# A neighbour-quantile graph kernel: other instructions for the degree classes, another direction of the stepped access in the long lists' keys, and two list steps on ScalarE instead of VectorE

## The chip, the cores and the metric

The kernel runs on one core of a Trainium2 chip. The metric is the device time of one execution in microseconds (us); lower is better. The engines are called as in the profile: PE is TensorE (PEld its weight loads), DVE is VectorE, ACT is ScalarE, POOL is GpSimd, SP is SyncE.

## What is computed

There are 16 graphs of 1024 nodes with 64 channels, a weighted adjacency of 1024 x 1024 for each, and two layers. The first adds a degree-normalised product of the adjacency with the normalised features. The second drops some neighbours, takes weighted quantiles over those that stay, for every node and channel, and puts the result through a two-layer MLP:

```python
h = jnp.maximum(_layernorm(x, axis=-1), 0.0)
x = x + _L0_gnn_ref(h, adj)            # (adj / clip(rowsum, 1)) @ h
h = jnp.maximum(_layernorm(x, axis=-1), 0.0)
x = x + _L1_gnn_ref(h, adj, nodemask, W1, b1, W2, b2)

# inside _L1_gnn_ref
nb = (adj_ > 0) & (~eye)[None]
m = nb.sum(-1)
rank = jnp.cumsum(nb, axis=-1) - 1
skip = jnp.where(m > T_THRESH, (m + K_DIL - 1) // K_DIL, 1)
removed = nb & do_dil[..., None] & ((rank + 1) % skip[..., None] == 0)
rem = removed | jnp.swapaxes(removed, 1, 2)
adj_d = jnp.where(rem, 0.0, adj_)
agg = _weighted_nanquantile_agg(x, adj_d > 0)    # quantiles 0.25, 0.5, 0.75 with weights 0.25, 0.5, 0.25
out = x + agg
h = jax.nn.relu(jnp.einsum('bnc,ch->bnh', out, W1) + b1)
y = (jnp.einsum('bnh,ho->bno', h, W2) + b2) * mask
```

The adjacency is sparse: most nodes have fewer than 16 neighbours, a few have up to some 90.

## The kernel before

**List path.** Sorting 1024 values for every node and channel would be wasteful, so the kernel makes a list of neighbours for every node, gathers their feature rows, and sorts the gathered values with a network of pairwise minima and maxima on DVE. A second path for dense graphs (`dense_path`) stands behind a condition and isn't taken with these inputs.

**First stage, a batch (graph) at a time.** The adjacency rows come in by DMA (`at`). ACT takes their sign with a row sum (`sg`, `total`). DVE multiplies the sign with a descending key and takes the eight largest keys in each of four segments (`rec`, 32 entries of a row, a 0 where there is none). PE transposes the rows and multiplies them with the features, ACT and DVE normalise. Then `endings` sorts the nodes of the batch by the length of their lists. Each node gets a class `d` from 0 to 22: below 16 it is the number of entries found; above, one more for each limit in `STEPS` that `total` passes; a full segment of eight makes it at least 16. The class is compared with a table of all classes (`cls`) to a one-hot `hot` of 23 x 8 entries, and PE products and a scan on DVE turn `hot` into places. POOL then scatters the rows of the nodes to these places in DRAM (`srt`) by indirect DMA.

**Second stage, a group at a time.** `GROUPS` makes four groups of four batches. `group(g)` reads the sorted records, drops the neighbours that the rule removes, and opens a `Job` for each class of lists: 15, 10 and 8 entries (one tile of 128 nodes each), 7 (two tiles), 6 (one tile), and 5 to 1 entries (four to six tiles). A job gathers one neighbour of 128 nodes with each indirect DMA on POOL (`places<-tab,idx`; for the last group `places<-tab,last_idx`). `sort` then finds the dropped places by comparison (`rem`, `gone`, `ok`), adds 1e30 times `gone` to their values in one DVE instruction so that they sort to the end, and runs the passes of the network. ACT takes the absolute value and the rectifier of the weights (`wu`, in `steps`). `weigh` multiplies the sorted values, which stand in one of two buffers (`places` is copy 0, `other` is copy 1), with the weights on DVE, one instruction for each run of places. For a short list the products go into `prod`. PE sums them by products with an identity (`pt`), then come the MLP on PE and ACT, one addition a tile on DVE (`y`), and a scatter to the output on POOL. The last group's tiles have names with `last_`; its jobs start once all batches are through.

**Long lists.** Eight rows of each batch have lists of up to 88, 28, 21 and 18 entries (`LONG`). `long_lists` makes, for each of the four, a row of keys in 16 bits (`lkey`): 1024 descending keys (`rev`) where the adjacency is positive, else 0. The instruction reads in the order of the columns and writes into eight segments, so that consecutive elements lie 128 elements, 256 bytes, apart. Searches in the segments (`lfound`, `lkeys`) give the indices for the gathers (`lplaces<-whole,lidx`). The first of the four (tag `l0`) is sorted in blocks by code of its own (`parts`, `merge`).

**Order of work.** It is written out at build time by a planner. Every piece of work is a Python generator (a stream) that yields the engine that it wants next, and when its inputs are ready. `Plan.run` always takes the stream that can start first by its own clocks and ranks; `Plan.note` moves the clocks by a cost for each instruction. A DVE instruction costs 0.07 us + 1.04 ns an element in it, an ACT instruction 0.06 us + 0.86 ns an element + 0.11 us for each bias or scale that is a pointer. The planner knows nothing of steps in memory. `SLACK` (2 us), `LOOSE` (7) and `LATE` (14) are distances that it leaves between a result and its reader. On the chip each engine runs its instructions in the written order[...].

In the trace nearly all instructions carry line 240, the planner's recording helper, so they are told apart by tile names.

Of the kernel before, what the change touches and what calls it, by code (L numbers as in the profile page):

```python
# [26 lines left out]

GROUPS = (4, 4, 4, 4)
NSEG = 4
STEPS = (16, 19, 22, 29, 39, 59, 79)  # L30
CLS = 15 + len(STEPS) + 1

# [353 lines left out]
def list_path(ctx, tc, x, adj, nodemask, w1, b1, w2, b2, out, go):  # L386
# [51 lines left out]
    nc.vector.memset(zero_f, 0.0)  # L438
    place1 = consts.tile([P, P], F32, name="place1")
    nc.vector.tensor_scalar(place1, col[:, :P], 1.0, None, op0=OP.add)  # L440
    cls_i = grp.tile([P, N], I32, name="gat_rows", bufs=1)[:, :CLS * NT]
    cls_i = cls_i.rearrange("p (c t) -> p c t", t=NT)
    nc.gpsimd.iota(cls_i, pattern=[[-1, CLS], [0, NT]], base=CLS - 1, channel_multiplier=0)
    cls = consts.tile([P, CLS, NT], F32, name="cls")
    nc.vector.tensor_copy(cls, cls_i)
    row_i = consts.tile([P, NT], I32, name="row_i")
    nc.gpsimd.iota(row_i, pattern=[[P, NT]], base=0, channel_multiplier=1)
    row_f = consts.tile([P, NT], F32, name="row_f")
# [323 lines left out]
    def endings(pool, now):  # L772

        first = lambda rank: rank - 3000
        for b, st in enumerate(batch):
            now[0] = b
            g = max(g for g in range(NG) if FIRST[g] <= b)
            size = GROUPS[g]
            yield "ACT", lambda: known(st, "rec", "row") if st["listed"] == NT else INF
            rec, total, row = st["rec"], st["total"], st["row"]  # L780

            for t in range(NT):
                nc.scalar.activation(
                    row[:, t, R0:R0 + 8 * NSEG], rec[:, t, :], AF.Relu, bias=before[:, t:t + 1]
                )


            yield "DVE", always
            found = new(pool, [P, NT, 8 * NSEG], BF, "found", 1)
            nc.vector.tensor_scalar(found, rec, 0.0, None, op0=OP.is_gt)  # L790
            d = new(tiny, [P, NT], F32, "d", 2)
            nc.vector.tensor_reduce(d, found, AX.X, OP.add)
            full = new(tiny, [P, NT], F32, "full", 2)
            nc.vector.tensor_reduce(
                full, found.rearrange("p t (s e) -> p t s e", e=8)[:, :, :, 7], AX.X, OP.max
            )
            nc.vector.scalar_tensor_tensor(d, full, float(STEPS[0]), d, op0=OP.mult, op1=OP.max)
            nc.vector.tensor_scalar(d, d, float(STEPS[0]), None, op0=OP.min)
            for s in STEPS[1:]:
                nc.vector.scalar_tensor_tensor(d, total, float(s), d, op0=OP.is_gt, op1=OP.add)  # L800
            free(rec)
            free(total)
            hot = new(tiny, [P, CLS, NT], BF, "hot", 2)
            nc.vector.tensor_tensor(
                hot, cls, d.unsqueeze(1).to_broadcast([P, CLS, NT]), OP.is_equal
            )
            yield "PE", lambda: max(at(hot), room("ps_small", 3))
            pc = new(ps_s, [P, HALF], F32, "ps_small", 3, users=1)
            K = CLS * NT
# [12 lines left out]
            pos = new(tiny, [P, NT], F32, "pos", 2)  # L822
            nc.vector.tensor_reduce(pos, base.rearrange("p (c t) -> p t c", t=NT), AX.X, OP.add)
            low = new(tiny, [P, NT], I32, "low", 2)
            nc.vector.tensor_copy(low, pos)
            nc.vector.tensor_scalar(low, low, LSUB - 1, None, op0=OP.bitwise_and)
            if size == 2:
                aside = new(tiny, [P, 2, NT], F32, "aside", 2)
                for e, by in enumerate((-32.0, 64.0)):
                    nc.vector.tensor_scalar(  # L830
                        aside[:, e, :], pos, 64.0 / (e + 1), by, op0=OP.is_lt, op1=OP.mult
                    )
                for e in range(2):
# [12 lines left out]
            progress["batches"] = b + 1  # L846
# [23 lines left out]
    class Job:  # L870
# [185 lines left out]
        def steps(self):  # L1056
            nc.scalar.activation(self.u, self.u, AF.Abs)
            nc.scalar.activation(self.u, self.u, AF.Relu, bias=wt0, scale=-QUANTILES[0][1])

        def merge(self):  # L1060
            self.counts(self.ok)
            yield "ACT", lambda: at(self.u) + SLACK
            self.steps()
            yield "DVE", always, self.later
            yield from self.passes(len(self.ops) - 1, self.landed)
            yield from self.weigh()

        def sort(self):
# [14 lines left out]
            self.ops, self.count, self.copies = network(n, T * C, one=T == 1)  # L1083
            self.counts(ok)

            vals = A[:, 1:, :, :].rearrange("p k t w -> p (k t) w")[:, :, :C]
            nc.vector.scalar_tensor_tensor(
                vals,
                gone.rearrange("p k t -> p (k t)").unsqueeze(2).to_broadcast(
                    [P, (n - 1) * T, C]  # L1090
                ),
                HUGE, vals, op0=OP.mult, op1=OP.add,
            )
            free(gone)
            yield "ACT", lambda: at(self.u) + SLACK
            self.steps()
            yield "DVE", lambda: max(
                room("prod", 2) if short else 0.0,
                room(name + "other", 1),
            ), self.later  # L1100
            if short:
# [8 lines left out]
        def weigh(self):  # L1110
# [12 lines left out]
            if short:  # L1123
                prod = new(pool, [P, T, total, C], F32, "prod", 2, users=1)
                if count + 1 < total:
                    nc.vector.memset(prod[:, :, count + 1:, :], 0.0)

            for copy in (1, 0):
                mine = [k for k in range(count) if copies[k] == copy]
                for run in runs_of(mine):  # L1130
                    first, step, number = run[:3]
                    sl = slice(first, first + step * (number - 1) + 1, step)
                    src = places(copy, run)
                    nc.vector.tensor_tensor(
                        prod[:, :, sl, :].rearrange("p t k c -> p k t c") if short else src, src,
                        w[:, sl, :].unsqueeze(3).to_broadcast([P, number, T, C]), OP.mult,
                    )
            if short:
                free(A)
                free(Bt)  # L1140
                yield "ACT", lambda: at(S)
                nc.scalar.copy(prod[:, :, count, :], S[:, :, :C])
                free(S)

                terms = [
                    [prod[:, t, k:min(k + 2, total), :].rearrange("p k c -> p (k c)")
                     for k in (0, *range(4, total, 2), 2)]
                    for t in range(T)
                ]
                plan.add(self.layers(terms, [prod]), self.urgent)  # L1150
            else:
                terms = [[places(copies[k], (k, 1, 1, 1, 1))[:, 0, 0, :] for k in range(count)]
                         + [S[:, 0, :C]]]
                plan.add(self.layers(terms, [A, Bt]), -1000)
# [278 lines left out]
    def long_lists(pool):  # L1433

        yield "DVE", always
        rev = new(pool, [P, N], HF, "rev", 1)
        nc.vector.tensor_scalar(rev, col_f, -1.0, float(N), op0=OP.mult, op1=OP.add)
        yield "SP", always
        place = new(pool, [P, 1], I32, "lplace", 1)
        nc.vector.tensor_scalar(place, part, 7, None, op0=OP.bitwise_and)  # L1440
# [17 lines left out]
        for l in LORDER:  # L1458
# [17 lines left out]
            key = new(pool, [P, N], HF, "lkey", 1)  # L1476
            segs = key.rearrange("p (s q) -> p s q", s=LSEG)
            nc.vector.scalar_tensor_tensor(
                segs.rearrange("p s q -> p q s"), full.rearrange("p (q s) -> p q s", s=LSEG), 0.0,
                rev.rearrange("p (q s) -> p q s", s=LSEG), op0=OP.is_gt, op1=OP.mult,  # L1480
            )

            found = new(pool, [P, LSEG, max(LCAPS)], HF, "lfound", 1)
# [395 lines left out]
```

## Time and profile before

| what | value |
|---|---|
| median of 3 runs | 1413.34 us (1410.7 to 1415.0) |
| profiled execution | 1414.18 us, span 1412.4 us |
| DVE busy | 1228.7 us (87%), 4150 instructions |
| POOL busy | 963.8 us (68%), 1115 instructions |
| PE busy | 738.8 us (52%) |
| ACT busy | 557.6 us (39%), 1603 instructions |
| chain that ended last | DVE 46%, POOL 18%, issue 10%, PE 10%, DMA 9%, ACT 6% |

The first stage runs to about 860 us, with the groups' work mixed in from 195 us on; the rest is the remaining groups and the long lists. In the rows of the profile, `out<-in` names the tiles, `xN` is the number of instructions, then come the busy time in us, the mean in ns of one, and the idle time of the engine just before them with what ended it. "issue" is time in which an engine waited for nothing that the profile shows.

### The profile page before, as it was taken

To read this page: it belongs to the slowest core of one execution; us is meant where nothing else is said; L and a number is where in the kernel's file an instruction comes from. 1 tells how busy PE (TensorE), PEld (TensorE's weight loads), DVE (VectorE), ACT (ScalarE), POOL (GpSimd) and SP (SyncE) were. 2 spreads that over 40 slices of the span, in tenths; PEclk is the share of its full clock that TensorE was granted. 3 is DMA by queue.
4 is the path that set the end of the run, shared out by engine and by line. 5 is a ranking of instruction groups with operands and counts; after the bars stand their busy time and mean duration, and the time that the engine had idled before them with its cause. 6 is when DMAs were issued, how large, how long until landed. Compare 5 with 4: busy or idle time off the path is not lost.

```text
span 1412.4 us, 14420 instructions
## 1 busy us (share of the span) xinstructions
PE 738.8 (52%) x3203; PEld 458.2 (32%) x3203; DVE 1228.7 (87%) x4150; ACT 557.6 (39%) x1603; POOL 963.8 (68%) x1115
## 2 busy tenths in 40 slices
PE   4878726376677657839856652002002232337685
PEld 2434413243443335425442331001001121226455
DVE  6999898999888898998999668886998899998985
ACT  6889763765554356865653520000000110001010
POOL 0042347777775787776778877775877777787764
PEclk9999868687787868968966865555555555557566
DMA  5464582443444245545541324211111111111110
GB/s 174 156 195 163 182 228 76 133 154 90 124 107 136 69 119 170 150 142 148 158 125 46 85 46 84 73 44 46 32 25 24 25 34 26 25 28 40 25 25 16
DMA packets 133834, 132.31 MB, mean 94 GB/s; under 512 B 99444, under 2 KB 102132, under 8 KB 133620
## 3 DMA queue, kind: packets, MB, share of 16 engines
q1 hardware_dynamic: 102220, 91.13, 21.8%
q0 software_dynamic: 31520, 40.19, 11.7%
q8 instruction: 27, 0.44, 0.1%
q14 instruction: 67, 0.55, 0.1%
HBM read 111.76 MB, written 23.61 MB: 96 GB/s over the span
## 4 chain that ended last, share of the span: by engine, by line
DVE 46%; POOL 18%; issue 10%; PE 10%; DMA 9%; ACT 6%; SPq 0%; DVEq 0%; POOLq 0%; ACTq 0%
POOL places L240 14%; DVE places L240 8%; DVE rec L240 6%; DVE other L240 5%; PE ps_small L240 5%; PE pt L240 5%; DVE lplaces L240 4%; DVE sg L240 2%; DMA at<-in_adj_dram 2%; DMA places<-tab,idx 2%; DVE l0other L240 2%; ACT sg L240 2%; POOL srt L240 2%; DVE prod L240 2%; DVE lkey L240 1%
## 5 line engine op out<-in xcount | busy, mean ns | idle before, releaser
L240 POOL DMA_INDIRECT places<-tab,idx x372 | 375.8, 1010 | 121.2 <-issue 104.2
L240 PE MATMUL pt<-ident,prod 128*128 128x128 f32 (+1 forms) x736 | 152.2, 367 | 385.8 <-DVE prod L240 330.9
L240 PE MATMUL ps_small<-att,h 128*65 128x512 f32 x512 | 261.7, 662 | 77.3 <-ACT h L240 55.9
L240 PEld LDWEIGHTS pt<-ident,prod 128*128 128x128 f32 (+1 forms) x736 | 126.0, 252 | 418.0 <-DVE prod L240 248.6
L240 POOL DMA_INDIRECT srt<-row,to x128 | 131.6, 1028 | 140.0 <-ACT row L240 118.9
L240 PE MATMUL pt<-ident,at 128*128 128x128 f32 x1024 | 164.0, 304 | 72.0 <-ACT att L240 52.7
L240 DVE MAX8 rec<-sg 128x8 f16<-128x256 f16 x512 | 180.2, 414 | 4.4
L240 ACT ACTIVATE sg<-at 128x1024 f16<-128x1024 f32 x128 | 134.8, 1054 | 102.0 <-DMA at<-in_adj_dram 65.6
L240 POOL DMA_INDIRECT lplaces<-whole,lidx x125 | 146.8, 1174 | 38.1 <-issue 36.9
L240 ACT COPY ot<-pt 128x128 f32<-128x128 f32 (+3 forms) x56 | 22.4, 400 | 377.4 <-PE pt L240 377.2
L240 PEld LDWEIGHTS pt<-ident,at 128*128 128x128 f32 x1024 | 125.7, 155 | 113.9 <-ACT att L240 77.6
L240 POOL DMA_INDIRECT places<-tab,last_idx x124 | 135.0, 1089 | 37.8 <-issue 35.0
L240 ACT COPY att<-pt 128x512 f32<-128x512 f32 x256 | 140.7, 584 | 26.8 <-PE pt L240 25.3
L240 PEld LDWEIGHTS ps_small<-att,h 128*65 128x65 f32 x512 | 76.1, 155 | 220.9 <-issue 125.0
L240 POOL DMA_INDIRECT out_dram<-y,nodes_i x93 | 95.7, 1029 | 20.6 <-issue 12.7
L240 DVE TENSOR_TENSOR sg<-sg,keyed 128x1024 f16<-128x1024 f16 x128 | 87.4, 682 | 15.6 <-ACT sg L240 15.6
L240 ACT ACTIVATE wu<-wu 128x39 f32<-128x39 f32 (+9 forms) x40 | 9.4, 235 | 152.0 <-DVE wu L240 152.0
L240 PE MATMUL ps_small<-ot,w_sb 128*128 128x128 f32 (+3 forms) x112 | 52.0, 554 | 30.8 <-DVE base L240 11.9
L240 DVE TENSOR_TENSOR places<-places,other 128x128 f32<-128x128 f32 (+6 forms) x160 | 56.4, 355 | 3.4
L240 PE MATMUL ps_small<-w_sb,hid 128*128 128x64 f32 x256 | 50.1, 332 | 1.9 <-ACT hid L240 1.6
L240 DVE TENSOR_TENSOR places<-other,places 128x128 f32<-128x128 f32 (+5 forms) x136 | 48.8, 366 | 1.7
L240 DVE TENSOR_TENSOR other<-places 128x256 f32<-128x256 f32 (+4 forms) x124 | 48.1, 388 | 1.9
(292 smaller groups left out, 1600.7 us busy)
## 6 DMA issues: line engine op xcount, KB each, us to landing
at<-in_adj_dram SPq DMA_DIRECT2D x64, 1024.0 KB, 5.6
places<-tab,idx POOLq DMA_INDIRECT x372
whole<-tab SPq DMA_DIRECT2D x4, 1057.0 KB
tab<-row SPq DMA_DIRECT2D x16, 264.0 KB, 3.8
xt<-in_x_dram SPq DMA_DIRECT2D x16, 256.0 KB, 6.7
S<-srt SPq DMA_DIRECT2D x12, 192.0 KB, 2.6
y<-srt SPq DMA_DIRECT2D x12, 192.0 KB, 2.7
srt<-row,to POOLq DMA_INDIRECT x128
```

The lines of the kernel that those rows point to most:

```text
L240: ins = getattr(self._engine, op)(*args, **kwargs)
```

## The change

1. In `endings` the class is no longer counted. `STEPS` holds all 22 limits from 1 up, `total` is raised to 17 where a segment is full, one comparison with a table of 24 limits (`limits`, made once by 24 memsets in place of `cls`) gives `above`, and the difference of neighbouring rows is `hot`.
2. In `long_lists` the keys are written contiguously, and the adjacency row is read with a step of 8 elements (32 bytes) instead. `rev` is made in this order once.
3. A job is `helped` if it belongs to the last group or to the three shorter long lists, has one tile, and if ACT's planned clock is less than 2 us ahead of DVE's. Then ACT multiplies `gone` by 1e30 and adds it to the values with one instruction for each place, and in `weigh` ACT multiplies place by place with the weights (for short lists only those in copy 0).

```diff
-STEPS = (16, 19, 22, 29, 39, 59, 79)
-CLS = 15 + len(STEPS) + 1
+STEPS = (*range(1, 17), 19, 22, 29, 39, 59, 79)
+CLS = len(STEPS) + 1
...
-    nc.gpsimd.iota(cls_i, pattern=[[-1, CLS], [0, NT]], base=CLS - 1, channel_multiplier=0)
-    cls = consts.tile([P, CLS, NT], F32, name="cls")
-    nc.vector.tensor_copy(cls, cls_i)
+    limits = consts.tile([P, CLS + 1, NT], F32, name="limits")
+    for c, limit in enumerate((HUGE, *reversed(STEPS), -HUGE)):
+        nc.vector.memset(limits[:, c, :], float(limit))
...
-            found = new(pool, [P, NT, 8 * NSEG], BF, "found", 1)
-            nc.vector.tensor_scalar(found, rec, 0.0, None, op0=OP.is_gt)
-            d = new(tiny, [P, NT], F32, "d", 2)
-            nc.vector.tensor_reduce(d, found, AX.X, OP.add)
             full = new(tiny, [P, NT], F32, "full", 2)
             nc.vector.tensor_reduce(
-                full, found.rearrange("p t (s e) -> p t s e", e=8)[:, :, :, 7], AX.X, OP.max
-            )
-            nc.vector.scalar_tensor_tensor(d, full, float(STEPS[0]), d, op0=OP.mult, op1=OP.max)
-            nc.vector.tensor_scalar(d, d, float(STEPS[0]), None, op0=OP.min)
-            for s in STEPS[1:]:
-                nc.vector.scalar_tensor_tensor(d, total, float(s), d, op0=OP.is_gt, op1=OP.add)
+                full, rec.rearrange("p t (s e) -> p t s e", e=8)[:, :, :, 7], AX.X, OP.max
+            )
+            nc.vector.tensor_scalar(full, full, 0.0, 17.0, op0=OP.is_gt, op1=OP.mult)
+            nc.vector.tensor_tensor(total, total, full, OP.max)
             free(rec)
+            above = new(tiny, [P, CLS + 1, NT], BF, "above", 1)
+            nc.vector.tensor_tensor(
+                above, total.unsqueeze(1).to_broadcast([P, CLS + 1, NT]), limits, OP.is_gt
+            )
             free(total)
             hot = new(tiny, [P, CLS, NT], BF, "hot", 2)
-            nc.vector.tensor_tensor(
-                hot, cls, d.unsqueeze(1).to_broadcast([P, CLS, NT]), OP.is_equal
-            )
+            nc.vector.tensor_tensor(hot, above[:, 1:, :], above[:, :CLS, :], OP.subtract)
...
+        def helped(self):
+            return (
+                self.g >= NG - 1 and self.tag != "l0" and self.T == 1
+                and plan.clock["ACT"] < plan.clock["DVE"] + 2.0
+            )
...
+            helped = self.helped()
+            if helped:
+                yield "ACT", lambda: at(gone) + SLACK
+                nc.scalar.mul(gone, gone, HUGE)
+                for t in range(T):
+                    for k in range(1, n):
+                        if (t or k > 1) and k % 4 == 1:
+                            yield "ACT", always
+                        val = A[:, k, t, :C]
+                        nc.scalar.activation(val, val, AF.Identity, bias=gone[:, k - 1, t:t + 1])
+            else:
...
+            helped = self.helped()
             for copy in (1, 0):
                 mine = [k for k in range(count) if copies[k] == copy]
+                if helped and (copy == 0 or not short):
+                    yield "ACT", lambda: at(w) + SLACK
+                    for e, k in enumerate(mine):
+                        if e and e % 4 == 0:
+                            yield "ACT", always
+                        for t in range(T):
+                            src = places(copy, (k, 1, 1, 1, 1))[:, 0, t, :]
+                            nc.scalar.activation(
+                                prod[:, t, k, :] if short else src, src, AF.Copy,
+                                scale=w[:, k, t:t + 1],
+                            )
+                    continue
...
-        nc.vector.tensor_scalar(rev, col_f, -1.0, float(N), op0=OP.mult, op1=OP.add)
+        nc.vector.tensor_scalar(
+            rev.rearrange("p (s q) -> p s q", s=LSEG),
+            col_f.rearrange("p (q s) -> p s q", s=LSEG), -1.0, float(N), op0=OP.mult, op1=OP.add,
+        )
...
             nc.vector.scalar_tensor_tensor(
-                segs.rearrange("p s q -> p q s"), full.rearrange("p (q s) -> p q s", s=LSEG), 0.0,
-                rev.rearrange("p (q s) -> p q s", s=LSEG), op0=OP.is_gt, op1=OP.mult,
+                segs, full.rearrange("p (q s) -> p s q", s=LSEG), 0.0,
+                rev.rearrange("p (s q) -> p s q", s=LSEG), op0=OP.is_gt, op1=OP.mult,
             )
```

More of the change, by code (lines that the diff above doesn't have):

```diff
@@ L440, in list_path @@
     nc.vector.tensor_scalar(place1, col[:, :P], 1.0, None, op0=OP.add)
-    cls_i = grp.tile([P, N], I32, name="gat_rows", bufs=1)[:, :CLS * NT]
-    cls_i = cls_i.rearrange("p (c t) -> p c t", t=NT)
-    nc.gpsimd.iota(cls_i, pattern=[[-1, CLS], [0, NT]], base=CLS - 1, channel_multiplier=0)
-    cls = consts.tile([P, CLS, NT], F32, name="cls")
-    nc.vector.tensor_copy(cls, cls_i)
+    limits = consts.tile([P, CLS + 1, NT], F32, name="limits")
+    for c, limit in enumerate((HUGE, *reversed(STEPS), -HUGE)):
+        nc.vector.memset(limits[:, c, :], float(limit))
     row_i = consts.tile([P, NT], I32, name="row_i")
@@ L1084, in sort @@
             self.counts(ok)
[L1086 to L1092, printed above, removed]
-            )
+            helped = self.helped()
[9 more added lines that the diff above has]
+            else:
+                vals = A[:, 1:, :, :].rearrange("p k t w -> p (k t) w")[:, :, :C]
+                nc.vector.scalar_tensor_tensor(
+                    vals,
+                    gone.rearrange("p k t -> p (k t)").unsqueeze(2).to_broadcast(
+                        [P, (n - 1) * T, C]
+                    ),
+                    HUGE, vals, op0=OP.mult, op1=OP.add,
+                )
             free(gone)
@@ L1097, in sort @@
             yield "DVE", lambda: max(
-                room("prod", 2) if short else 0.0,
+                at(A) + SLACK if helped else 0.0, room("prod", 2) if short else 0.0,
                 room(name + "other", 1),
@@ L1140, in weigh @@
                 free(Bt)
-                yield "ACT", lambda: at(S)
+                if not helped:
+                    yield "ACT", lambda: at(S)
                 nc.scalar.copy(prod[:, :, count, :], S[:, :, :C])
```

## The prediction

> **What bounds the kernel now.** I read the page's busy row by slices first: whether one engine is full over the whole span.
>
> ```profile
> DVE  6999898999888898998999668886998899998985
> ACT  6889763765554356865653520000000110001010
> POOL 0042347777775787776778877775877777787764
> ...
> DVE 46%; POOL 18%; issue 10%; PE 10%; DMA 9%; ACT 6%; SPq 0%; DVEq 0%; POOLq 0%; ACTq 0%
> ```
>
> Each digit is a fortieth, 35 us. DVE stands at 8 to 9 tenths almost everywhere. POOL stands at 7 to 8 from the sixth slice on, and that is fuller than it looks: after each gather its queue shows 0.30 us of "issue". A gather costs 0.94 us at best plus 0.30, so 80 gathers in 100 us fill it. The waits of POOL between 195 us (first gather) and 1361 us (last) sum to some 202 us of issue, and only about 40 us of waiting for DVE (base 10.0, lnodes_i 9.3, nodes 8.4, gbasep 7.5). So two engines are nearly full at once, and the last line, the chain that ended last, changes between them: DVE 46%, POOL with its issue gaps 28%. ACT is nearly idle from 900 us on (36 us busy of 512).
>
> Next, the timeline of all engines around one key-making instruction of the long lists:
>
> ```profile
> 933.27 1.28 DVE L240 SCALAR_TENSOR_TENSOR gat_rows<-col_f,lS,gat_rows 128x1024 f32<-128x1024 f32 x1 [1.71 <-DMA gat_rows<-in_adj_dram,lnodes_i]
> 933.57 1.80 POOL L240 DMA_INDIRECT lplaces<-whole,lidx  x1 [0.30 <-issue]
> 934.59 4.70 DVE L240 SCALAR_TENSOR_TENSOR lkey<-gat_rows,rev 128x1024 f16<-128x1024 f32 x1
> 935.68 3.94 POOL L240 DMA_INDIRECT lplaces<-whole,lidx  x1 [0.31 <-issue]
> ```
>
> Two instructions over the same 1024 elements take 1.28 and 4.70 us; the second writes with a step of 256 bytes. And the gather issued inside it takes 3.94 us instead of 0.94: it ends when DVE's instruction ends. Long DVE work costs POOL time too.
>
> Last, the groups of DVE and ACT that the change touches:
>
> ```profile
> L240 DVE SCALAR_TENSOR_TENSOR lkey<-gat_rows,rev 128x1024 f16<-128x1024 f32 x4 | 18.8, 4700 | 0.1
> L240 DVE SCALAR_TENSOR_TENSOR d<-total,d 128x8 f32<-128x8 f32 x96 | 16.0, 167 | 3.3
> L240 DVE TENSOR_REDUCE d<-found 128x8 f32<-128x256 bf16 x16 | 6.7, 420 | 0.5
> L240 DVE TENSOR_REDUCE pos<-base 128x8 f32<-128x184 f32 x16 | 7.8, 484 | 0.6
> L240 DVE TENSOR_TENSOR hot<-cls,d 128x184 bf16<-128x184 f32 x16 | 5.6, 352 | 0.5
> ...
> L240 DVE SCALAR_TENSOR_TENSOR lplaces<-lgone,lplaces 128x1792 f32<-128x1792 f32 x1 | 2.0, 2017 | 0.0
> ...
> L240 DVE TENSOR_TENSOR lplaces<-lplaces,lw 128x1344 f32<-128x1344 f32 x1 | 1.6, 1552 | 0.0
> ```
>
> The 96 tiny steps of 167 ns are the classes; the last two rows are work that goes to ACT.
>
> [...] the reduction pos reads 184 elements 32 bytes apart in 484 ns, some 1.8 ns each after 150 ns of fixed cost; the stepped write costs 4.70/1024 = 4.6 ns[...]. [...] The trace has 343 ns for 60 elements with a pointer bias. [...] the trace shows two table loads in all, so I add none for Identity and Copy.
>
> **The change, part by part.** Durations are of the profiled execution, 1414.18 us with a span of 1412.4; the median of the runs is 1413.34, 0.06% below.
>
> *Classes.* Removed per batch: found 0.22, d 0.42, full 0.20, two steps 0.34, six steps of 0.167, hot 0.35. In the timeline of batch 0 they hold DVE from 40.42 to 43.12, 2.70 us. Added: full on rec (32 elements, 0.20), two steps of 8 elements (0.17 each), above (192 elements in f32, 0.36 by the old hot), hot in 16-bit types (estimate 0.25, from sg's 682 ns for 1024), less overlaps: 1.15 us. It saves 1.55 us x 16 = 24.8 us of DVE. But the chain passes through these steps in only 5 of 16 batches and through half of them in one: 5.5 x 1.55 = **8.5 us** on the path. The others lie under POOL's queue, the adjacency loads or the PE. Bounds 0 and 24.8. At the start 24 memsets replace an iota and a cast; a row of 32 such memsets took 0.48 us there, and DVE then waits 8.3 us for the PE: nothing.
>
> *Keys.* The write becomes contiguous, the f32 read steps 32 bytes. With pos's 1.8 ns: 1.84 + 0.1 = 1.9 us; from below 1.28 (gat_rows, contiguous)[...]. Saved 2.8 us (2.1 to 3.4). Three of four keys lie on the chain themselves (934, 968, 991 us: gather, key, search, indices, next gather). The first, at 891, is on it through POOL's 3.94 us gather at 892.78, which loses about as much. 4 x 2.8 = **11.2 us**. The constant rev, 694 ns, reads with a step too: +**1.2**, once.
>
> *Lists on ACT.* The condition holds wherever ACT's planned clock is not 2 us ahead of DVE's; with ACT idle there I take it as true for all seven lists (15, 10, 8 and 6 entries of the last group; 28, 21, 18). DVE loses four drops of 1149, 817, 697 and 551 ns, three of 2017, 1551 and 1351, two weightings of short lists (1.25 together) and five of long ones (4.4): 13.8 us in 14 instructions. ACT gains 39 + 67 additions, 7 products with HUGE and 14 + 54 weightings, 181 instructions x 0.24 = 43 us, into more than 400 idle us. From 1000 to 1300 about 40% of the chain is POOL and its issue; later gathers also end DVE's waits. So I count 40% of the 13.8: **5.5 us** (0 to 13.8).
> The added waits: DVE's first compare of such a list waits for ACT's last addition (up to 28 x 0.24 = 6.7 us); queued behind it on DVE are the passes of the other lists and the y additions. The planner knows of the wait and puts other passes first: that work hides it. PE waits for ACT's last product. For the 18-entry list, last in the trace, nothing hides this: place 0 comes last on ACT and first on PE. Its weighting took 1.3 us on DVE (1395.8 to 1397.1) and takes 15 x 0.24 + 0.2 = 3.8: +**2.5 us** at the end, bounds 0 (another list ends last) and 4.
>
> Sum: -8.5 - 11.2 + 1.2 - 5.5 + 2.5 = -21.5, so 1414.2 - 21.5 = 1392.7; I say **1392**. What is late next is POOL: its gathers don't get fewer.
>
> **The rivals.**
> *POOL paces all.* For it: POOL waited only 40 us in 1166. Then of the classes only the two endings on the chain before the first gather count (3.1 us), the keys give 11.2 (POOL is held by them), the lists nothing, with 1.2 and 2.5 against: -10.6, **1404**. Against it: DVE fills 46% of the chain.
> *DVE paces all.* -24.8 - 11.2 + 1.2 - 13.8 + 2.5 = -46, **1368**. Against it: DVE waits for gathers until 1302, 1328 and 1346.
> *The condition seldom holds.* Then only classes and keys count: -18.5, **1396**. Against it: ACT's zeros in the slices.
> *DVE stands in line for ACT* (slower). Instructions on DVE run in the written order. If the planner finds nothing to put ahead, the additions (106 x 0.24 + 7 x 0.22 = 27 us) stop DVE in full, and the products (16.3 against 5.6 us) lie on the path: +37.7 instead of -3, with the other parts -18.5: +19, **1433**. It turns slower once over half of the 43 us is exposed. For it: y stood 11.5 us for PE at 955, so the order doesn't always hide a chain. Against it: from 1000 to 1300 DVE was 93% busy with passes that are free to go first.
>
> **How the numbers follow.** My forecast 0.52, POOL paces 0.22, DVE paces 0.12, condition fails 0.06, in line for ACT 0.08. The planner writes a new order everywhere, which moves each case by several us. 0.3%, 4 us, is about what a measurement of this kernel can tell from no change. Nearly all of the forecast and of DVE paces is below 1409, and most of POOL paces: faster 0.86; within 0.3%: 0.05; slower 0.09. The range leaves out the tail of the slow case and a little at the bottom: 1366 to 1411.
>
> **What would show it.** Right: lkey near 1.9 us and no gather of 3.9 us beside it; the classes at some 1.15 us a batch; ACT rows places<-places,gone of about 0.25 to 0.33 us; DVE's busy time down from 1229 by some 48 us (24.8 + 10 + 13.8). Wrong: lkey above 2.6 us; DVE rows waiting for ACT's places or lplaces by more than 20 us in sum; a first gather no earlier than 195 us; an ACT row with two pointer costs, near 0.43.

## The result, and the profile after

After the change the kernel takes 1420.14 us (median of 14 runs, 1415.58 to 1421.93) against 1414.01 us before (14 runs, 1410.70 to 1417.73): a ratio of 1.0036, 95% interval 1.0025 to 1.0048. It is 6.1 us slower, where 1392 was forecast. The profiled execution of the change took 1416.59 us, with a span of 1414.4. Each run below is compared with runs of the kernel before on its own chip. Ten of the eighteen runs fell on two other chips, on which the kernel before itself took 1792 to 1817 us, and they stand apart at the end of the experiments. Medians are of all runs, ratios of those that lie within 1.5% of the fastest of their kernel.

The page of the kernel after first: busy time, and the slices of DVE, ACT and POOL, a fortieth of the span each.

```profile
PE 741.1 (52%) x3203; PEld 463.5 (33%) x3203; DVE 1185.8 (84%) x4047; ACT 600.8 (42%) x1784; POOL 948.4 (67%) x1120
...
DVE  6987987999658999897998667785997999999791
ACT  6877866465635845666572531000000414011321
POOL 0043237777747778778778677775877777877843
```

DVE lost 42.9 us of work (1228.7 before), ACT gained 43.2, and the span did not get shorter. ACT now works in slices from 1096 us on where it had zeros and ones. In the last slice DVE falls from 5 to 1, and PE and POOL end the kernel.

The groups of the kernel after, with different shapes kept apart (count, then busy us, mean ns of one, idle time before them):

```profile
L240 ACT ACTIVATE lplaces<-lplaces,lgone 128x64 f32<-128x64 f32 x67 | 16.4, 333 | 0.1
L240 ACT ACTIVATE lplaces<-lplaces,lw 128x64 f32<-128x64 f32 x39 | 9.9, 334 | 3.5 <-DVE lw L240 3.5
L240 ACT ACTIVATE places<-places,gone 128x64 f32<-128x64 f32 x39 | 9.7, 335 | 0.1
L240 DVE SCALAR_TENSOR_TENSOR lkey<-gat_rows,rev 128x1024 f16<-128x1024 f32 x4 | 8.0, 1988 | 0.1
...
L240 DVE TENSOR_TENSOR above<-total,limits 128x192 bf16<-128x192 f32 x16 | 5.7, 358 | 0.5
...
L240 DVE TENSOR_TENSOR hot<-above 128x184 bf16<-128x184 bf16 x16 | 4.2, 261 | 0.6
...
L240 DVE TENSOR_REDUCE full<-rec 128x8 f32<-128x32 f16 x16 | 3.2, 201 | 0.0
```

Most sizes of the prediction are here: the key at 1.99 us (1.9 foreseen), `above` 358 ns (360), `hot` 261 (250), an addition on ACT 333 ns alone and, from its busy time, 16.4 / 67 = 0.245 us in a row (0.24). All 39 + 67 additions are on ACT, so the condition held for every list.

The timeline of the kernel after around the second long list's key:

```profile
937.21 1.32 DVE L240 SCALAR_TENSOR_TENSOR gat_rows<-col_f,lS,gat_rows 128x1024 f32<-128x1024 f32 x1 [1.96 <-DMA gat_rows<-in_adj_dram,lnodes_i]
937.27 0.94 POOL L240 DMA_INDIRECT lplaces<-whole,lidx  x1 [0.30 <-issue]
938.52 0.94 POOL L240 DMA_INDIRECT lplaces<-whole,lidx  x1 [0.30 <-issue]
938.56 1.99 DVE L240 SCALAR_TENSOR_TENSOR lkey<-gat_rows,rev 128x1024 f16<-128x1024 f32 x1
939.76 1.56 POOL L240 DMA_INDIRECT lplaces<-whole,lidx  x1 [0.31 <-issue]
```

The gather beside the key takes 1.56 us instead of 3.94. So most of the small work was priced well, and the question is where the time went. Two places in the trace of the kernel after stand out. The first is POOL's wait of 18.5 us for DVE's `gbasep` near 423 us (in the kernel before, its longest wait between the first and the last gather was 10.0). The second is the end. The timeline of the kernel after, from the last long list's weights on:

```profile
1380.48 3.45 ACT L240 ACTIVATE lother<-lother,lw 128x64 f32<-128x64 f32 x14 [13.57 <-DVE lw L240]
...
1383.83 0.33 ACT L240 ACTIVATE lplaces<-lplaces,lw 128x64 f32<-128x64 f32 x1
1384.22 0.69 PE L240 MATMUL pt<-ident,lplaces 128*64 128x128 f32 x2 [7.18 <-ACT lplaces L240]
...
1390.74 1.60 PE L240 MATMUL pt<-ident,prod 128*128 128x128 f32 x12
...
1394.42 0.28 DVE L240 SCALAR_TENSOR_TENSOR y<-ps_small,lS 128x64 f32<-128x64 f32 x1 [12.26 <-PE ps_small L240]
...
1394.99 0.96 POOL L240 DMA_INDIRECT out_dram<-y,lnodes_i  x1 [13.00 <-DVE y L240]
...
1396.25 0.96 POOL L240 DMA_INDIRECT out_dram<-y,last_nodes_i  x1 [0.19 <-issue]
...
1408.91 0.96 POOL L240 DMA_INDIRECT out_dram<-y,last_nodes_i  x1 [0.19 <-POOLq L380]
```

DVE makes the last weights (`lw`) at 1380.3, 15 us earlier than before (1395.4). Then PE stands 7.18 us for ACT's last product, with a sum of the last group (`prod`) queued behind, and POOL stands 13.00 us at the scatter of the last long list. Eleven scatters of the last group follow, one every 1.27 us. Eight of their tiles had been ready on DVE since 1382.2; they stand behind in POOL's queue. The kernel before ends differently:

```profile
1397.51 0.96 POOL L240 DMA_INDIRECT out_dram<-y,lnodes_i  x1 [9.84 <-DVE y L240]
...
1398.77 0.96 POOL L240 DMA_INDIRECT out_dram<-y,last_nodes_i  x1 [0.19 <-issue]
...
1405.66 0.96 POOL L240 DMA_INDIRECT out_dram<-y,lnodes_i  x1 [0.77 <-DVE bad L1591]
```

There POOL waits for the third long list, five scatters follow, and the last long list goes out last.

**An account of POOL.** The span is cut at POOL's first gather (`places<-tab,idx`) and the end of its last (`places<-tab,last_idx`). All kernels of this table issue 838 indirect DMAs in that stretch, and it is the sum of POOL's busy time, the gaps of up to 0.6 us, and the longer idle time within it, all read from POOL's timeline. The kernels are those of the experiments. Two executions of nearly one order (the change, and the change with its end turned) differ by 1.7 us in the first gather and 3.7 in the stretch, so a single row is good to no better than that.

| kernel (one execution) | first gather | stretch | busy | gaps | idle | end | span |
|---|---|---|---|---|---|---|---|
| before | 194.8 | 1166.7 | 900.7 | 234.4 | 32.3 | 50.9 | 1412.4 |
| keys alone | 195.0 | 1156.2 | 888.2 | 234.8 | 33.9 | 50.4 | 1401.6 |
| classes alone, old order | 193.7 | 1167.2 | 899.2 | 234.6 | 33.9 | 49.5 | 1410.4 |
| classes alone, own order | 196.8 | 1173.3 | 904.4 | 234.5 | 35.2 | 50.4 | 1420.5 |
| lists alone | 194.1 | 1165.3 | 895.2 | 234.0 | 36.7 | 59.8 | 1419.2 |
| lists alone, end turned | 192.6 | 1163.8 | 894.5 | 234.5 | 35.4 | 47.5 | 1403.9 |
| after | 198.6 | 1155.7 | 885.7 | 233.9 | 36.6 | 60.1 | 1414.4 |
| after, end turned | 200.3 | 1159.4 | 890.2 | 234.2 | 35.8 | 48.2 | 1407.9 |
| all parts, old class order, end turned | 193.8 | 1151.6 | 885.5 | 234.4 | 32.3 | 48.9 | 1394.3 |

(A few MEMSETs and rounding make the small remainders. "End" is what follows the last gather; first gather, stretch and end add up to the span.) POOL stands idle for only some 32 to 37 us of about 1160 in every kernel, so it is nearly full between its first and its last gather.

### The profile page after: what moved, and what is told of

The parts are those of the page before. It is cut to its first block, busy times and chain, and to the rows that moved or that the text cites. A ratio compares the mean times of both kernels' runs of the same rounds, so it can differ in the third digit from the quotient of the medians.

```text
span 1414.4 us, 14549 instructions
## 1 busy us (share of the span) xinstructions
PE 741.1 (52%) x3203; PEld 463.5 (33%) x3203; DVE 1185.8 (84%) x4047; ACT 600.8 (42%) x1784; POOL 948.4 (67%) x1120
## 5 line engine op out<-in xcount | busy, mean ns | idle before, releaser
L240 POOL DMA_INDIRECT places<-tab,idx x372 | 375.7, 1010 | 119.5 <-issue 106.7
L240 PE MATMUL pt<-ident,prod 128*128 128x128 f32 (+1 forms) x736 | 155.8, 373 | 403.2 <-DVE prod L240 368.6
L240 PE MATMUL ps_small<-att,h 128*65 128x512 f32 x512 | 255.8, 647 | 22.7 <-DVE y L240 10.6
L240 PE MATMUL pt<-ident,at 128*128 128x128 f32 x1024 | 176.6, 318 | 88.6 <-ACT att L240 61.1
L240 PEld LDWEIGHTS pt<-ident,at 128*128 128x128 f32 x1024 | 134.2, 162 | 136.6 <-ACT att L240 89.5
L240 POOL DMA_INDIRECT lplaces<-whole,lidx x125 | 135.7, 1085 | 38.1 <-issue 37.2
L240 POOL DMA_INDIRECT places<-tab,last_idx x124 | 131.3, 1059 | 37.8 <-issue 35.1
L240 PE MATMUL ps_small<-ot,w_sb 128*128 128x128 f32 (+3 forms) x112 | 47.9, 517 | 21.4 <-ACT ot L240 16.2
L240 PE MATMUL ps_small<-w_sb,hid 128*128 128x64 f32 x256 | 49.5, 331 | 5.0 <-ACT hid L240 4.7
L240 DVE TENSOR_TENSOR places<-other,places 128x128 f32<-128x128 f32 (+5 forms) x136 | 48.9, 367 | 1.8
```

The lines of the kernel that those rows point to most:

```text
L240: ins = getattr(self._engine, op)(*args, **kwargs)
```

## The experiments

**1. Keys alone.** Only the two hunks of the keys; the written order is that of the kernel before.

```diff
-                segs.rearrange("p s q -> p q s"), full.rearrange("p (q s) -> p q s", s=LSEG), 0.0,
-                rev.rearrange("p (q s) -> p q s", s=LSEG), op0=OP.is_gt, op1=OP.mult,
+                segs, full.rearrange("p (q s) -> p s q", s=LSEG), 0.0,
+                rev.rearrange("p (s q) -> p s q", s=LSEG), op0=OP.is_gt, op1=OP.mult,
```

> The kernel before with the second part alone: keys and rev read with a step, written contiguously. The planner costs both forms alike, so every engine's order stays as before. Theory (the keys lie on the chain, the gain was given back elsewhere): lkey near 1.99 us instead of 4.70, and the time falls by 8 to 13 us (ratio 0.991 to 0.994). Rival (a shorter key only lengthens a wait for a gather or for PE, so the part is worth nothing): within 3 us of before.

Measured: 1402.96 against 1412.78 us, ratio 0.9924 (0.9910 to 0.9939): 9.8 us faster. The groups of this kernel:

```profile
L240 POOL DMA_INDIRECT lplaces<-whole,lidx x125 | 138.1, 1105 | 38.1 <-issue 37.8 <-DVE l0other L240 0.3
L240 DVE SCALAR_TENSOR_TENSOR lkey<-gat_rows,rev 128x1024 f16<-128x1024 f32 x4 | 7.9, 1986 | 0.1
...
L240 DVE TENSOR_SCALAR rev<-col_f 128x1024 f16<-128x1024 f32 x1 | 1.1, 1093 | 4.7 <-DMA srt<-row,to 4.7
```

A gather of the long lists takes 1105 ns in the mean against 1174 before: 125 x 0.069 = 8.6 us of POOL's queue. In the account POOL's busy time in the stretch falls by 12.5 us and the stretch by 10.5. So the gain shows on POOL; how much of it came through the gathers that the key held and how much through DVE's own chain, these runs don't tell apart.

**2 and 3. Classes alone, in two orders.** Both run the class hunks of the change. In the first the planner is told nothing of the new steps but is charged for the old ones, step by step, so that the order of all else should stay as before. In the traces POOL's order does, and DVE's but for a few neighbours; on PE, ACT and SP some instructions stand in other places all the same. In the second it is charged by its formula, as in the change.

```diff
+            raw = tc.nc.vector          # the new steps, past the planner
+            raw.tensor_reduce(full, ...)
...
+            plan.clock["DVE"] = ...     # the formula's time of the old steps
```

> The kernel before with the first part alone (one comparison for the classes), but the planner is charged for the old, longer steps, so that every other instruction stands in its old order on every engine. Theory (in the first stage DVE isn't what sets the pace; the adjacency loads, PE and ACT and POOL's queue are): the 25 us that DVE saves are worth 0 to 4 us. Rival (my forecast: 5.5 of 16 batches have these steps on the chain): 7 to 10 us faster.

Measured: 1409.44 us, ratio 0.9976 (0.9965 to 0.9987): 3.3 us faster. DVE is 21.6 us less busy (1207.1), so most of what it saved became waiting. (The profiled execution, 1412.54 us, is 3.1 us above the median, so its row of the account can't show where the 3.3 us came from.)

> The kernel before with the first part alone, as in the change, so that the planner writes a new order from the cheaper classes. Theory (the new order loses in the first stage what the shorter steps give: the last batch's one-hot came at 829 us instead of 825, the long lists' first key at 898 instead of 892): 2 to 8 us slower than the same part in the old order, so between -2 and +6 us against before. Rival (the order is neutral): equal to the run in the old order within 2 us.

Measured: 1421.93 us, ratio 1.0066 (1.0048 to 1.0084): 9.2 us slower. The same instructions in the order that the change's own costs bring are 12.5 us slower than in the old order, more than the 2 to 8 expected. The first place that stands out in the traces is the start of group 1. The timeline of the old order:

```profile
411.89 0.89 SPq L240 DMA_DIRECT2D recs<-srt  x2
...
413.81 0.21 DVE L240 TENSOR_SCALAR hnodes<-recs,noff 128x1 f32<-128x1 f32 x1 [4.08 <-DMA recs<-srt]
...
415.83 0.98 POOL L240 DMA_INDIRECT gat_rows<-in_adj_dram,hnodes_i  x1 [0.31 <-DVE keys L240]
...
430.17 0.96 POOL L240 DMA_INDIRECT tab<-drop,didx  x1 [10.81 <-DVE base L240]
```

And of the own order:

```profile
401.26 0.88 SPq L240 DMA_DIRECT2D recs<-srt  x2
402.19 2.81 SPq L240 DMA_DIRECT2D S<-srt  x1
405.18 2.71 SPq L240 DMA_DIRECT2D y<-srt  x2
407.98 0.45 SPq L240 DMA_DIRECT2D at<-in_adj_dram  x1
...
413.08 1.06 ACT L240 ACTIVATE sg<-at 128x1024 f16<-128x1024 f32 x1 [17.38 <-DMA at<-in_adj_dram]
...
414.26 0.69 DVE L240 TENSOR_TENSOR sg<-sg,keyed 128x1024 f16<-128x1024 f16 x1 [14.51 <-ACT sg L240]
...
421.98 0.21 DVE L240 TENSOR_SCALAR hnodes<-recs,noff 128x1 f32<-128x1 f32 x1
...
422.64 0.98 POOL L240 DMA_INDIRECT gat_rows<-in_adj_dram,hnodes_i  x1 [17.71 <-DVE gbasep L240]
...
436.24 0.99 POOL L240 DMA_INDIRECT tab<-drop,didx  x1 [0.30 <-DVE keys L240]
```

The faster classes bring batch 7's last scatter 10 us earlier (it ends at 399.9, in the old order at about 410). So group 1's loads (`recs`, `S`, `y`) come earlier on SP, ahead of an adjacency pair, which goes out only at 407.98. ACT waits 17.38 us for it, DVE waits 14.51 for ACT's sign, and group 1's first steps stand behind this row, the one after it and the end of the ninth batch on DVE. POOL is empty for 17.71 us, and the group's dropped places (`tab<-drop`) go out at 436 instead of 430. An input that came 10 us earlier made the group's start 6 us later.

But this place doesn't account for the 12.5 us. The old order waits here too, 10.81 and 4.3 us, and again 3.8 us at the start of group 2, where the own order doesn't. Counted by POOL's indirect DMAs, the own order is 1.7 us behind at the 180th (near 385 us), 7.1 at the 240th, only 2.6 at the 380th (near 670), and 10.5 at the 500th (near 830), about as much as at the 800th (9.8). So most of the loss arises between 670 and 830 us. There POOL's instructions take longer in the own order (the indirect DMAs 1028 ns in the mean against 997), and POOL waits once for the rows of a batch; the timeline of the own order:

```profile
810.59 1.00 POOL L240 DMA_INDIRECT srt<-row,to  x1 [3.95 <-ACT row L240]
```

**4. The end turned.** The change as it is, but the planner leaves 30 us instead of 7 between the last long list's weights and its PE sum, so that the last group's sums and scatters stand ahead of it. Only the last few dozen instructions change their order.

```diff
+LAST = 30.0
...
-                at(*sources) + LOOSE, room("pt", 2),
+                at(*sources) + (LAST if self.n == LONG[3] + 1 else LOOSE), room("pt", 2),
```

> The changed kernel, where the PE sum of the last long list (18 entries) is planned 30 us behind its values instead of 7. Only the last few dozen instructions change places: that list's row leaves POOL as the last of 16 scatters and not ahead of 11 others. Theory (the end gives back what DVE gained: POOL waits 13.0 us for this list's y with finished rows behind it, and then needs 11 x 1.27 us): 8 to 14 us faster than the changed kernel, so 0.993 to 0.998 of before. Rival (the end is set by the chain of the list on ACT and PE, and the scatters hide in any order): within 3 us of the changed kernel.

Measured: 1407.34 us, ratio 0.9955 (0.9942 to 0.9968) to before, where the change has 1.0036: some 11 us for the order of the last scatters.

**5. Lists alone.** Only the hunks of the lists.

> The list part alone again, where the kernel before takes about 1413 us. Theory (POOL's queue paces; the end is lost through the order of the last scatters): the stretch from first to last gather 3 to 8 us shorter than 1166.7, the end behind it 59 to 61 instead of 50.9 us, the time 0 to 6 us longer than before. Rival 1 (the forecast's 5.5 us saved and 2.5 lost): 3 us shorter. Rival 2 (DVE stands in line for ACT in the middle too): over 10 us longer, with the stretch itself longer.

Measured: 1419.08 against 1412.83 us, ratio 1.0036 (1.0022 to 1.0049): 6.3 us slower, a little over what the theory had. The stretch fell by 1.4 us only; the end grew from 50.9 to 59.8.

**6. Lists alone, with the end turned** by the edit of experiment 4.

> The list part alone, with the last long list's PE sum planned 30 us instead of 7 behind its weights, so that the eleven last scatters of the last group do not stand behind that list's scatter. Theory: the end is 48 to 51 us again, and the time is 9 to 12 us under that of the list part with its own order at the end: 3 to 9 us shorter than before. Rival (what holds the end is ACT's time for the weights of the last list, not the place of its scatter): the end stays above 57 us, within 3 us of the list part with its own order.

Measured: 1406.88 us, ratio 0.9957 (0.9940 to 0.9974): 6.0 us faster than before and 12.2 under experiment 5. The timeline of this kernel:

```profile
1381.42 3.45 ACT L241 ACTIVATE lother<-lother,lw 128x64 f32<-128x64 f32 x14 [13.84 <-DVE lw L241]
...
1383.12 0.96 POOL L241 DMA_INDIRECT out_dram<-y,last_nodes_i  x1 [0.19 <-DVE y L241]
...
1388.48 5.42 PE L241 MATMUL pt<-ident,lother 128*64 128x128 f32 x26
...
1395.74 0.96 POOL L241 DMA_INDIRECT out_dram<-y,last_nodes_i  x1 [0.19 <-issue]
...
1397.00 0.95 POOL L241 DMA_INDIRECT out_dram<-y,lnodes_i  x1 [0.19 <-DVE go L1627]
```

ACT's products take the same 3.45 us. While ACT, PE and DVE finish the last list, POOL sends eleven tiles of the last group, and the list's own scatter comes last with no wait. So ACT's time for the weights was not what held the end; the place of this list's sum and scatter was.

**7. All three parts, classes in the old order, end turned.** Edits of 1, 2, 4 and 5 together.

> All three parts, with the planner charging the class steps as it did the old ones, and the end turned, where the kernel before takes about 1413 us. Theory (each part is worth what it gave alone): keys 10, classes 3, lists 5, end 1 us shorter: about 1394, ratio 0.984 to 0.989. Rival (the parts share one slack, POOL's, which the keys use up): no better than the keys alone, ratio 0.992 or more.

Measured: 1396.34 us, ratio 0.9881 (0.9861 to 0.9900): 16.5 us faster than before and some 22 under the change, each against its own runs of the kernel before, with the same work done by the same instructions. The parts alone gave 9.8 + 3.3 + 6.0 = 19.1 us, so they nearly add up; the rival of one shared slack falls. Of the kernels measured here this is the fastest.

**8. Another order of the classes.** Classes alone, the new steps charged 1.7 us in all. (The expectation gives the other charges as 0.8 and 2.5; with the 0.15 us that the planner leaves between dependent steps, its formula comes to about 1.4 for the new steps and 3.1 for the old.)

```diff
+            plan.clock["DVE"] = max(plan.clock["DVE"], ...) + 1.7
```

> The classes alone, with the planner charging the new steps 1.7 us of DVE, where the kernel before takes about 1413 us. Group 1 starts on DVE behind 78 keyed rows and eight finished batches, as before. Theory (the 12 us of the new order come from the place of group 1's start behind a ninth batch's ending and waiting rows): POOL's wait near 420 us is under 8 us instead of 18, the time 1407 to 1413. Rival (any other order of the first stage loses about as much): 1416 to 1424, with the loss at other places.

Measured: 1417.07 us, ratio 1.0030 (1.0019 to 1.0041): 4.2 us slower than before, 4.9 under the own order. The theory missed, and the time is in the rival's range. Group 1's start is ahead of the ninth batch's ending here, and POOL waits even longer, in three stops of 9.02, 11.79 and 2.38 us:

```profile
425.74 0.69 DVE L240 TENSOR_TENSOR sg<-sg,keyed 128x1024 f16<-128x1024 f16 x1 [13.29 <-ACT sg L240]
...
432.50 0.97 POOL L240 DMA_INDIRECT gat_rows<-in_adj_dram,hnodes_i  x1 [9.02 <-DVE gbasep L240]
...
446.54 0.96 POOL L240 DMA_INDIRECT tab<-drop,didx  x1 [11.79 <-DVE gfound L240]
```

The start is behind rows that wait for ACT, as in experiment 3, and the dropped places go out at 446.5, 10 us later than there. Yet the kernel is no slower: the two profiled executions took 1421.9 and 1422.2 us, the median is 4.9 us lower. A later start of group 1 doesn't make a longer time by itself. This speaks against that start as the main cause of the 12.5 us, and agrees with the rival that another order loses at other places.

**9. On two other chips.** The first eight rows of the table are of one chip, at two times: the kernel before took 1817 us beside the first four and 1792 beside the next four. The last two rows are of another, where it took 1817. The waits of the first of these kernels look different:

```profile
PE pt L240 <- issue: 407.3, 48, 120.2
...
ACT att L240 <- remote: 200.4, 30, 19.7
```

PE stood 407 us in 48 stops for nothing that the profile shows, up to 120.2 us at a time (115 to 383 us in the other nine), and POOL was idle 457 us between its first and last gather instead of 32. The granted TensorE clock was 0.65 to 0.67 in the profiled executions, on the chips of experiments 1 to 8 it was 0.71 to 0.72. POOL, nearly full there, is not full here, so none of these ratios decides a theory. Rows with the same edit as an experiment above carry nearly the same expectation.

| kernel | median, us | ratio (95%) |
|---|---|---|
| lists alone (5) | 1817.84 | 1.0011 (0.9988 to 1.0034) |
| all parts, old class order, end turned (7) | 1806.23 | 0.9930 (0.9906 to 0.9955) |
| classes charged 1.7 us (8) | 1821.17 | 1.0022 (0.9999 to 1.0044) |
| classes, rows later | 1822.64 | 1.0013 (0.9983 to 1.0042) |
| classes, group 1 first | 1822.72 | 1.0161 (1.0117 to 1.0205) |
| after, both places mended | 1806.01 | 1.0082 (1.0054 to 1.0110) |
| classes, rows later, again | 1801.06 | 1.0059 (1.0036 to 1.0082) |
| classes charged 1.2 us | 1807.31 | 1.0062 (1.0035 to 1.0090) |
| classes, group 1 first, again | 1846.86 | 1.0165 (1.0131 to 1.0199) |
| after, both places mended, again | 1831.85 | 1.0077 (1.0053 to 1.0101) |

"Group 1 first" holds the keyed rows back in the written order while a start is pending, "rows later" puts 6 us between sign and product, and "both places mended" is the change with group 1 first and the end turned:

```diff
-                    at(st["signs"][t]) + SLACK if t in st["signs"] else INF, ...
+                    INF if progress["starting"] else at(st["signs"][t]) + SLACK if ...
...
-                    at(st["signs"][t]) + SLACK if t in st["signs"] else INF, ...
+                    at(st["signs"][t]) + 6.0 if t in st["signs"] else INF, ...
```

> The classes alone with the order of the change, but keyed rows are held back in the written order while group 1's start is pending: its first DVE steps stand ahead of the two rows that wait for ACT's signs, not behind them. Theory (that place costs most of the 12 us): POOL's wait of 17.7 us near 420 us falls below 8 us, group 1's dropped places go out near 428 instead of 436 us, and the time is 1408 to 1415 instead of 1421.9. Rival (the place is one of many, and the lost time shows up elsewhere): POOL's wait goes, but the time stays at 1417 to 1423.

> The whole change with its own charge for the class steps, group 1's start ahead of the two waiting rows, and the last long list's PE sum planned 30 us behind its weights. Theory (the two places account for the loss): 1394 to 1402, ratio 0.987 to 0.992, near the 1396.3 of all parts with the old class order. Rival (only the end counts): within 2 us of the 1407.3 of the change with its end turned alone.

> The classes alone with the light charge of the change, but the planner leaves 6 us instead of 2 between ACT's sign of a row and DVE's product with it; group 1 starts behind 78 rows and eight batches. Measured where the kernel before takes about 1413 us. Theory (DVE's waits for ACT's signs, 37 us against 20 in the old order, are where the classes' 25 us went, and hold group starts): waits for sg below 20 us, time 1405 to 1413. Rival (they are only where DVE's slack shows): waits for sg fall, others grow as much, 1417 to 1424.

> The classes alone, with the planner charging the new steps 1.2 us of DVE in all, about what they take on the chip; the change charges 0.8, the old steps were charged 2.5. In this order group 1 starts behind 74 rows and nine batches. Theory (an order is good or bad by single places, not by how true the charge is): between 1409 and 1422, following POOL's wait near 420 us at about 0.6 us for each us of it. Rival (a true charge gives the best order): 1405 to 1410.

These expectations are for a chip on which the kernel before takes about 1413 us, and there the kernels of the last seven rows have not been measured. On the two chips here, the new orders lost 0.1 to 1.7%. That the order costs the 12.5 us is shown (experiments 2 and 3: the same instructions). By which places it does stays open: the chain through SP, ACT and DVE at group 1 is read from the trace, not tried, and experiment 8 and the count of POOL's DMAs speak against it as the main one. The granted clock was also a little lower in the own order (0.708 to 0.718 against 0.714 to 0.724 in its runs); whether that is a cause or follows from the order isn't shown.

## Why the prediction was wrong

**The sizes were close, but for one.** The key took 1.99 us (1.9 foreseen), the new class steps some 1.3 us a batch (1.15), an addition on ACT 0.245 us (0.24). The trace of the kernel before shows this figure too: its `ln_sq<-row,ln_s`, 64 elements with one pointer, takes 0.33 us, and ACT's next instruction begins 0.24 us after it began (322.18 and 322.42 us); `h<-xt,ln_s,ln_v`, 64 elements with two pointers, takes 429 ns. ACT has two table loads in the traces of both kernels, so its new work brought none. The constant `rev` cost 0.4 us more, not 1.2. DVE's busy time fell by 42.9 us of 48 foreseen.

**Keys: right.** Foreseen -11.2 + 1.2 = -10 us, measured -9.8 (8.6 to 12.7 by the interval). The path named, the keys themselves and the gathers that they held, fits the account. For the step of 32 bytes the prediction took 1.8 ns an element from `pos` in its own trace, (484 - 150)/184; the 150 ns is the author's estimate of what doesn't grow with the elements (that kernel's class steps of 8 elements took 167 ns). The key came to 1.94, fixed cost included. The limit of 2.6 us for the key was not read from a trace; the key stayed below it, at 1.99.

**Classes: the step that failed.** "5.5 x 1.55 = 8.5 us on the path" was mis-sized, and a term was missing. In nearly the old order the classes give 3.3 us (1.8 to 4.9 by the interval). The chain passing through an instruction doesn't make its time a gain: POOL, next in line, was almost as full: it had 32 us of idle time in a stretch of 1167. The rival "POOL paces all" had 3.1 us for the classes, and its mechanism is the one that the account supports, although a single execution can't place the 3.3 us before the first gather, as the rival did. The missing term is the order. The prediction put it down as "moves each case by several us", a spread with no sign. For the classes alone it was +12.5 us, and it took more than the gain; which places of the order cost it stays open. The check on the first gather had it right: 198.6 us is later than the 195 at which the prediction was to count as wrong.

**Lists: the sum right, its place in doubt.** Foreseen -5.5; with the end turned the list part gave -6.0 (3.7 to 8.5). In the account the stretch got 1.4 to 2.9 of this, no more than single rows differ by, and the end 3.4. What is clear lies behind the last gather: DVE's last weights come 25 to 26 us after it with the list part and 34 before. The prediction placed its gain between 1000 and 1300 us and took 40% from the chain; no run tests that share, so the agreement may be luck.

**The end: "+2.5, bounds 0 and 4" was the second failed step.** It priced ACT's 15 products in place of DVE's weighting, and forgot what stood behind the scatter of that list on POOL. The planner's new clocks put eleven scatters behind it, 11 x 1.27 = 14 us, in place of none. The difference between the two orders of the end was 12.2 us (experiments 5 and 6). The bound of 4 left it out: the prediction asked who waits for ACT, but not what waits behind it in the queue of POOL.

**The sum.** From the single parts as the change has them: keys -9.8, classes with their order +9.2, lists with their end +6.3, together +5.7; measured +6.1. From the same parts without the two orders: -19.1; measured together -16.5, or 1396.3 us. That this is not far from the 1392 forecast is in part luck: 5.2 us too much for the classes stand against the 2.5 at the end that the turned order didn't lose. Of the rivals, "DVE stands in line for ACT" ended on the right side for another reason: the trace of the change has no wait of DVE for ACT's products or additions. DVE's waits for `sg` grew instead (35.4 us between 200 and 860, 20.5 in the old order of experiment 2). Later loads don't explain that in sum: ACT waited 64 us for adjacency rows in the own order of experiment 3 and 77 in the old one.

## What to carry to other kernels

Where a program's order is written from modelled costs, a change of costs is a change of order, and it has a price of its own: run the new instructions once in the old order, and count the two apart. At the end of a kernel look at each queue and ask what stands behind the item that becomes ready last; put it last. Price a saving by the queue that is next in line, not by the chain alone: here 21.6 us of DVE were worth 3.3, and 11 us of DVE that also held POOL were worth 9.8.

## What the runs showed of the hardware

Turning the stepped access round gave the key 2.7 us and cost the constant `rev` little (1.09 us against 0.69). Over 1024 elements, fixed cost included, the key with two sources took 4.6 ns an element with a 16-bit write that steps 256 bytes, and 1.94 with an f32 read that steps 32 bytes; `gat_rows`, without a step, took 1.25. In `rev`, with one source, the same step of a read came to 1.07 ns an element. So one figure for a step doesn't fit both. A gather on POOL beside the key took 3.94 us when the key took 4.70, 1.56 beside 1.99, and 0.94 at best. In the kernel before, the gathers begun inside the four keys ended some 0.33 us after them. Gathers were longer beside some other long DVE instructions there too, but not beside all: a gather took 5.09 us beside the 4.55 us of `lplaces<-lplaces,l0w` (1259.5 us), and 0.94 and 0.95 beside two of 1.27 and 1.28 us, `gfound<-gat_rows,skip` (from 875 us on).

At the end of the kernel after, POOL kept to the written order: eight tiles of the last group were ready on DVE at 1382.2 us, and the first of their scatters began at 1396.25, behind the one for which POOL had stood 13.00 us.

On the two other chips two kinds of instruction on DVE and POOL were no longer (the new key took 1986 to 1988 ns, 1988 in the kernel after; a gather of the groups 979 to 997 ns, 1010 in the kernel before), while the kernel before took 27 to 29% longer. PE was busy for 771 to 811 us there (739 in the profile of the kernel before), and the rest lay between instructions; for part of these stops the profile shows no releaser. Why these chips are slower is not known.
